# Four graph layers in one launch: row blocks 0 to 2 of layer 3 moved into the end of layer 2

## The chip, the core and the metric

One core of a Trainium2 chip runs the whole program. Its engines work side by side and each takes its instructions in its own order: TensorE (PE, matrix products and transposes), VectorE (DVE), ScalarE (ACT), GpSimd (POOL) and SyncE (SP, which here only issues transfers). They wait for each other through semaphores. The metric is the time of one execution in microseconds (us), as the device measures it.

## The reference, cut to what matters

4096 nodes with 256 features, a dense 0/1 adjacency of 4096 x 4096, four graph layers; each is followed by a residual and a layer norm. The change touches the last two:

```
# layer 2, two steps: R is the row-normalised adjacency with a diagonal,
# A the attention of each row, cut to its top 90% of probability
for n in range(2):
    A  = top_p_attention(Xa, W1, W2, W3)
    Xf = R @ Xf
    Xa = A @ Xa
    Z  = Z + Xf @ U1[n].T + Xa @ U2[n].T
x = layernorm(x + layernorm(x0 + Z) * g + b)

# layer 3
agg = adj @ x / max(deg, 1)
x = layernorm(x + relu(concat([x, agg]) @ W + b))
```

Layer 3 is computed as adj @ (x W_low) and x W_high: the products with W come first, so that what is left per row block is one product of the adjacency with a matrix of 512 columns.

## The kernel before

The rows are taken in 32 blocks of 128. All blocks of one matrix fill one operand, XD, with a high and a low part of 256 columns each (their sum is the value); a product of the adjacency with it takes 32 matmuls of 128 x 128 by 512 for a row block.

Layer 2 runs two steps. In each, a loop over b pipelines several row blocks. For block b + 2 it makes the scores (logits and exponentials, `scores`) and the diffusion (`diffusion`, R @ Xf: eight pieces of the adjacency, 256 KB each, come from DRAM in three buffers, and each serves four matmuls with XD). For block b + 1 it finds the threshold of the attention (`nucleus`, nearly all of it on DVE) and masks the exponentials e with it (line 1145). For block b it turns the masked rows (`turn`, transposes, line 1285, with a copy on ACT) and multiplies them with X (`gather`, line 1294), eight times each. The exponentials of a block fill one of three tiles, e0 to e2, 16 KB on each partition. In step 1, `closing` (POOL, with statistics on DVE) makes h, the block's finished row after two layer norms, of the gathered sum, and `ahead3` multiplies h with the weights of layer 3 (`turned`, line 1378, and `weighted`, line 1387): the half for XD goes to DRAM as xtd, the other with h itself to xo. The order of TensorE, ACT, DVE and POOL in the loop is that in which the code is written out: eight stages s for each b. SP's order is made by a scheduler.

At the end of the loop (b = 30) no new block is begun. `settled` checks on DVE that every row's threshold is exact, and two small transposes (lines 1200 and 1204) bring the answer into one row of flags. It is stored to DRAM, and all engines read it back as a register. If a flag is not set, `mend` makes that block anew in an exact way; with these inputs that branch is not entered. The transposes stand in stage 4, ahead of the last gathers. Behind the loop, block 31 is turned and gathered, closed, and multiplied with the weights of layer 3. `reload` brings the finished rows of all other blocks from xtd into XD: seven loads of 1 MB for blocks 0 to 27, and one for 28 to 30. Block 31's own go from PSUM to XD (lines 1460 and 1462).

Layer 3 keeps the adjacency as bytes (nad) in DRAM. For each 8 row blocks, `bytes_of` loads four tiles of 1 MB over ACT's queue; `adj_pieces` casts them for one block, four pieces of 128 x 1024 by DVE (line 205) and ACT (line 203) in turn. Then come 32 matmuls (line 1647) and `close`: the sum over the degree, the bias, relu, residual and layer norm.

In step 1's diffusion the pieces are those that layer 1 stored, with a one added on the diagonal. The lines named L1158 and L1592 are those of the branch and of the flag's read.

Of the kernel before, what the change touches and what calls it, by code (L numbers as in the profile page):

```python
# [14 lines left out]
U8 = mybir.dt.uint8  # L15
# [40 lines left out]
class Net:  # L56
# [686 lines left out]
    def layer2(self):  # L743
# [3 lines left out]
        with ExitStack() as ctx:  # L747
            pool = ctx.enter_context(tc.tile_pool(name="l2", bufs=1))
            work = ctx.enter_context(tc.tile_pool(name="l2w", bufs=2))
            psum = ctx.enter_context(tc.tile_pool(name="l2ps", bufs=2, space=PSUM))  # L750
            ps1 = ctx.enter_context(tc.tile_pool(name="l2ps1", bufs=1, space=PSUM))
            dram = ctx.enter_context(tc.tile_pool(name="l2d", bufs=1, space=DRAM))
# [7 lines left out]

            es = [pool.tile([P, 4096], F32, name=f"e{i}") for i in range(3)]
            pre = es[0]
# [23 lines left out]
            nc.vector.memset(ones, 1.0)  # L786
            kT = pool.tile([P, N], F32R, name="kT")

# [136 lines left out]

            def product(q, out, **exp):

                e2 = out.rearrange("p (c n) -> p c n", n=1024)
                for c in range(HALF // 512):
                    pl = psum.tile([P, 2, 512], F32, name="ps_logit", bufs=2)  # L930
                    for s in range(2):
                        for t in range(2):
                            nc.tensor.matmul(pl[:, s, :], q[:, t, :], kT[:, (2 * c + s) * 512:(2 * c + s + 1) * 512],  # L933
                                             start=(t == 0), stop=(t == 1))
                    to = e2[:, c]
                    if exp:
                        nc.scalar.activation(to, pl.rearrange("p s n -> p (s n)"), AF.Exp, accum_out=exp["sums"][:, c:c + 1])  # L937
                    else:
                        nc.scalar.copy(to, pl.rearrange("p s n -> p (s n)"))
                    yield  # L940
# [21 lines left out]
            def scores(b, q):  # L962

                zp = small("zp", HALF // 512, bufs=2)
                yield from product(q, es[b % 3][:, :N], sums=zp)
                zj = small("zj", HALF // 512)
                nc.scalar.activation(zj, zp, AF.Identity, accum_out=Zs[:, b:b + 1])
# [186 lines left out]

            def mend(step, row, flag, e, r, h=None):


                with tc.If(flag == 0):  # L1158
                    with tc.For_i(0, NB - 1, 1) as b:
                        with tc.If(nc.values_load(row[:, at(b)], min_val=0, max_val=1) == 0):  # L1160
                            e2, Z = exact_scores(b)
                            r2 = exact_nucleus(e2, Z)
                            if step == 1:
                                finish(b, whole(closing(b, attention(e2), r2, bases(b))))
                            else:
                                store(b, attention(e2), r2)
                    with tc.If(nc.values_load(row[:, NB - 1:NB], min_val=0, max_val=1) == 0):
                        if step == 1:
                            e2, Z = exact_scores(NB - 1)
                            r2 = exact_nucleus(e2, Z)  # L1170
                            nc.scalar.mul(h[:, 0], attention(e2)[:, :D], r2)
                        else:
                            e2, Z = exact_scores(NB - 1, e)
                            nc.vector.tensor_copy(r, exact_nucleus(e2, Z))
                    if step == 1:
                        reload(xtd, 0, NB - 1)

            def settled():
# [18 lines left out]
                nc.vector.tensor_reduce(tmp, tto, AX.X, ALU.max)  # L1197
                nc.vector.scalar_tensor_tensor(ok, tmp, 0.0, ok, op0=ALU.is_equal, op1=ALU.mult)
                pt = psum.tile([P, 512], F32, name="ps_tp")
                nc.tensor.transpose(pt[:NB, :P], ok, self.ident)  # L1200
# [9 lines left out]

            def exact_scores(b, e=None):

                q = work.tile([P, 2, P], F32R, name="q", bufs=2)
                nc.sync.dma_start(q.bitcast(F32), qd[:, :, bass.ds(b * P, P)])
                if e is None:
                    e = es[(NB - 2) % 3][:, :N]
                whole(product(q, e))
# [253 lines left out]
            def weights(step):  # L1471
# [4 lines left out]
                nc.scalar.dma_start(affine, row_broadcast((self.ln_b, self.ln_g)[step], D))  # L1476

            weights(0)
            for step in range(2):
# [33 lines left out]
                with tc.manual_schedule(engines={ET.PE, ET.Activation, ET.DVE, ET.Pool}):  # L1513
                    for b in range(NB - 1):
                        ahead = b + 2 < NB
                        edge = nucleus(step, b + 1, *guess)
                        if ahead:
                            score = scores(b + 2, q)
                            beside = diffusion(step, b + 2)
                        close, kept, put = None, None, None  # L1520
                        for s in range(8):
                            if s == 0:
# [16 lines left out]
                            if step == 1 and b - 2 in done:  # L1539
# [3 lines left out]
                                elif s == 3:  # L1543
                                    pz = weighted(xT, pl[:, 1])
                            if ahead:
                                for _ in range(pieces[s]):
                                    next(beside)
# [31 lines left out]
                            if s == 4 and not ahead:  # L1579
                                row = settled()  # L1580
                            if s < 6:
                                aTs.append(turn(es[b % 3], s + 2))
                            elif ahead:
                                aTs.append(turn(es[(b + 1) % 3], s - 6))
                        if ahead:
                            pr = result(beside)
                            if b + 3 == NB:
                                reload((xfd, xtd)[step], 0, NB - 4)
# [28 lines left out]
                if step == 0:  # L1617
                    nc.scalar.mul(X[:, b, :], pa[:, :D], r)
                    reload(xfd, NB - 4, NB)
                else:  # L1620
                    hand = []
                    close = closing(b, pa, r, bases(b), hand.append)
                    next(close)
                    mend(step, row, flag, None, None, *hand)
                    reload(xtd, NB - 4, NB - 1)
                    finish(b, whole(close), True)

    def layer3(self):
        nc, tc, NB, D = self.nc, self.tc, self.NB, self.D
        G = 8
        with ExitStack() as ctx:
            pool = ctx.enter_context(tc.tile_pool(name="l3", bufs=1))
            work = ctx.enter_context(tc.tile_pool(name="l3w", bufs=2))
            psum = ctx.enter_context(tc.tile_pool(name="l3ps", bufs=4, space=PSUM))
# [6 lines left out]
            nas = []  # L1644

            def product(ps, a, jc):
                nc.tensor.matmul(ps, a[jc // G][:, jc % G, :], self.XD[:, jc].rearrange("p s d -> p (s d)"),  # L1647
                                 start=(jc == 0), stop=(jc == NB - 1))

            def products(b):  # L1650

                ps = psum.tile([P, 512], F32, name="ps_adj")
                a = pieces.pop(b)
                for jc in range(NB - 1):
                    product(ps, a, jc)
                return b, ps, a

            def close(b, ps, a, done=False):
                if not done:
                    product(ps, a, NB - 1)  # L1660
                x = work.tile([P, 2, D], F32, name="x", bufs=3)
# [11 lines left out]


            pieces = {b: self.adj_pieces(work, nas, b) for b in range(2)}
            first = [products(b) for b in range(2)]
            for t in first:
                close(*t)
                pieces[t[0] + 2] = self.adj_pieces(work, nas, t[0] + 2)
            for b in range(2, NB):  # L1680
                t = products(b)
                product(t[1], t[2], NB - 1)
                if b + 2 < NB:
                    pieces[b + 2] = self.adj_pieces(work, nas, b + 2)
                close(*t, done=True)

# [54 lines left out]
```

## Time and profile before

| what | value |
|---|---|
| median of 3 runs | 4110.43 us (4107.63 to 4112.28) |
| the profiled execution | 4113.95 us |
| its span, first to last instruction | 4112.3 us |
| TensorE: matmul busy, weight load busy | 3910.7 us, 3384.7 us |
| DVE, ACT, POOL busy | 3009.2, 2765.0, 1057.6 us |
| layer 3's matmuls, first to last | 3858.05 to 4098.62 us |
| bytes moved | 545.15 MB |

Times in the views count from the span's start. The three runs are of the unprofiled program, and the profiled execution is one more. A view of instructions in order of time gives the start, the busy time, and in brackets how long the engine had been idle before and what released it. A matmul of 32-bit floats is counted as two instructions, and as one where the operands are of the faster 32-bit kind (F32R), as all products with XD are.

### The profile page before, as it was taken

Reading aid. Unit: us, or ns where it says so; the run is one execution under the profiler, and the core shown is the slowest. Engines: PE = TensorE matmul, PEld = TensorE weight load, DVE = VectorE, ACT = ScalarE, POOL = GpSimd, SP = SyncE. Lnnn points to the kernel's source line nnn. Section 1 sums busy time; section 2 is a strip of 40 time slices with the busy share of each in tenths; the row PEclk is TensorE's granted clock in tenths of the full one; section 3 lists DMA queues with packets and bytes.
Section 4 is the critical chain, followed back from the end, with each engine's and each line's share of the span. In section 5 each row is a group of like instructions: output and inputs, shape, how many; then the busy total and the mean of one; then the engine's idle time right before and its main releaser. Section 6 shows DMA issues by size and latency. Waiting matters only on the chain. (4 is left out here: it accounts for less than half of the span.)

```text
span 4112.3 us, 68661 instructions
## 1 busy us (share of the span) xinstructions
PE 3910.7 (95%) x25081; PEld 3384.7 (82%) x25081; DVE 3009.2 (73%) x6659; ACT 2765.0 (67%) x5135; POOL 1057.6 (26%) x1297
## 2 busy tenths in 40 slices
PE   7999989999999899899999999988999999998798
PEld 6899989999999687468888888864888888887687
DVE  7642229999998344657888878846899999999254
ACT  5543339999997322458888888734888888886232
POOL 0111110110333122301111111103465555555110
PEclk9999999999999899899999999989999999999899
DMA  4765555324220597333333233444333333334431
GB/s 120 229 210 177 178 187 169 94 85 147 85 90 26 216 384 270 113 109 99 98 97 101 93 97 98 163 110 135 105 103 109 109 105 118 101 108 157 141 125 43
DMA packets 287962, 545.15 MB, mean 133 GB/s; under 512 B 38294, under 2 KB 118294, under 8 KB 283510
## 3 DMA queue, kind: packets, MB, share of 16 engines
q1 hardware_dynamic: 200068, 367.08, 27.8%
q10 hardware_dynamic: 61154, 93.25, 6.6%
q0 software_dynamic: 26384, 80.24, 5.9%
q8 instruction: 203, 3.33, 0.3%
q14 instruction: 153, 1.25, 0.1%
HBM read 374.51 MB, written 165.94 MB: 131 GB/s over the span
## 5 line engine op out<-in xcount | busy, mean ns | idle before, releaser
L1294 PE MATMUL ps_a<-X,aT 128*128 128x256 f32 x4096 | 974.6, 381 | 2.6 <-ACT h L1435 1.1
L1294 PEld LDWEIGHTS ps_a<-X,aT 128*128 128x128 f32 x4096 | 776.3, 191 | 127.0 <-issue 2.9
L300 PE MATMUL acc<-gm,gt 128*128 128x198 bf16 x8192 | 705.6, 249 | 26.7 <-issue 15.0
L300 PEld LDWEIGHTS <-gt 128*128 128x128 fp8e4 x8192 | 701.8, 97 | 30.4 <-issue 15.2
L292 ACT ACTIVATE sg<-lpb,nlc 128x1024 fp8e4<-128x1024 f32 x640 | 671.4, 1135 | 59.9 <-DVE gt L294 34.8
L179 PE MATMUL ps_r<-XD,adj_piece 128*128 128x512 f32 x2048 | 580.7, 418 | 10.0 <-ACT dif L1332 5.8
L517 PE MATMUL pz<-src,ar 128*128 128x264 f32 x4096 | 509.1, 287 | 11.7 <-DVE ar L507 9.1
L517 PEld LDWEIGHTS pz<-src,ar 128*128 128x128 f32 x4096 | 505.5, 189 | 15.2 <-DVE ar L507 12.8
L1030 ACT ACTIVATE ja<-e,nc 128x2048 uint8<-128x2048 f32 x240 | 480.9, 2004 | 2.0
L1287 ACT COPY aT<-ps_tp 128x512 f32<-128x512 f32 x512 | 295.9, 578 | 228.0 <-PE ps_tp L1285 218.4
L179 PEld LDWEIGHTS ps_r<-XD,adj_piece 128*128 128x128 f32 x2048 | 365.5, 191 | 91.2 <-issue 14.3
L510 ACT ACTIVATE nb<-a 128x512 uint8<-128x512 f32 x256 | 156.4, 630 | 292.4 <-DMA a<-in_adjt_dram 280.7
L1095 DVE MAX8 cand<-v 128x8 f32<-128x256 f32 x1024 | 347.2, 412 | 4.4
L203 ACT ACTIVATE adj_piece<-na 128x1024 fp32r<-128x1024 fp8e4 x128 | 135.3, 1059 | 318.9 <-PE ps_adj L731 134.6
L1145 DVE SCALAR_TENSOR_TENSOR e<-e,edge 128x512 f32<-128x512 f32 x512 | 345.9, 748 | 2.2
L1285 PE MATMUL ps_tp<-ident,e 128*128 128x128 f32 x2048 | 309.8, 274 | 5.3 <-ACTq L1158 3.9
L1285 PEld LDWEIGHTS ps_tp<-ident,e 128*128 128x128 f32 x2048 | 256.4, 141 | 59.0 <-ACTq L1158 4.3
L1091 DVE SCALAR_TENSOR_TENSOR v<-e,hi 128x2048 f32<-128x2048 f32 x128 | 301.9, 2359 | 2.3
L285 DVE TENSOR_SCALAR sg<-lpb,nlc 128x1024 fp8e4<-128x1024 f32 x384 | 283.0, 774 | 2.0
L933 PE MATMUL ps_logit<-kT,q 128*128 128x512 f32 x1024 | 274.7, 409 | 9.1 <-DVE kT L891 3.7
L937 ACT ACTIVATE e<-ps_logit 128x1024 f32<-128x1024 f32 x256 | 259.8, 1025 | 31.5 <-PE ps_logit L933 31.5
L507 DVE CAST ar<-a 128x1024 fp32r<-128x1024 f32 x128 | 88.7, 693 | 232.6 <-PE pz L517 232.3
(348 smaller groups left out, 5539.5 us busy)
## 6 DMA issues: line engine op xcount, KB each, us to landing
adj_piece<-adjs SPq DMA_DIRECT2D x512, 256.0 KB
a<-in_adjt_dram SPq DMA_DIRECT2D x256, 256.0 KB
adjs<-adj_piece SPq DMA_DIRECT2D x96, 512.0 KB
na<-nad SPq DMA_DIRECT2D x64, 512.0 KB
na<-nad ACTq DMA_DIRECT2D x32, 1024.0 KB
nad<-nb POOLq DMA_DIRECT2D x128, 128.0 KB, 3.3
lpb<-lpd POOLq DMA_DIRECT2D x32, 512.0 KB, 4.4
gmd<-gb ACTq DMA_DIRECT2D x64, 198.0 KB
```

The lines of the kernel that those rows point to most:

```text
L179: nc.tensor.matmul(ps, a[:, k, :], rhs(jc).rearrange("p s d -> p (s d)"), start=(jc == 0), stop=(jc == self.NB - 1))
L285: nc.vector.tensor_scalar(sg[:, k, :], lpb, nlc[:, jc, h:h + 1], 2.0 ** -5, op0=ALU.is_ge, op1=ALU.mult, saturate=False)
L292: nc.scalar.activation(sg[:, k, :], lpb, AF.Sign, scale=-1.0, bias=nlc[:, jc, h:h + 1], saturate=False)
L300: nc.tensor.matmul(acc[:, q, :6 * C1], gt[:, k, q * P:(q + 1) * P], gm[:, jc, hh, :], start=(jc == 0 and q % 2 == 0), stop=(jc == NB - 1 a ...
L517: nc.tensor.matmul(pz[q][:, t, :W], ar[:, q, k, :], src[:, jc, t, s], start=(jc == 0 and s == 0), stop=(jc == NB - 1 and s == 1))
L1030: nc.scalar.activation(ja, e[:, s * HALF:(s + 1) * HALF], f, bias=nc1, accum_out=fs[:, i + s:i + s + 1])
L1091: nc.vector.scalar_tensor_tensor(v, ec, hi, ec, op0=ALU.is_lt, op1=ALU.mult, accum_out=sb[:, s:s + 1])
L1095: nc.vector.max(cand[:, 8 * j:8 * j + 8], v[:, k * 256:(k + 1) * 256])
L1145: nc.vector.scalar_tensor_tensor(ec, ec, edge[:, j:j + 1], ec, op0=ALU.is_ge, op1=ALU.mult)
L1285: nc.tensor.transpose(pt[:, k * P:(k + 1) * P], e[:, jc * P:(jc + 1) * P], self.ident)
L1287: nc.scalar.copy(aT, pt)
L1294: nc.tensor.matmul(pa[:, :D], aT[:, k * P:(k + 1) * P], X[:, jc, :], start=(jc == 0), stop=(jc == NB - 1))
```

## The change

- The pools of layer 2 are split. e0 to e2 and kT stay on the left side of the memory and outlive layer 2, as do its PSUM pools; all others move to the right side.
- `settled` gives its DVE part in stage 4 and its transposes after the loop, in both steps.
- In the last iteration of step 1, `early` makes 28 of the 32 matmuls of layer 3's row blocks 0 and 1: two pieces of the adjacency in each stage from the second on. The pieces come over SP's queue, and POOL takes the one off the diagonal again.
- Behind the branch, block 2 is made in the same way, and `cast3` casts block 3 from bytes into kT, all by DVE. The order of this end is written out too. Block 31's last layer norm, its product and the last four matmuls, one of each block, follow.
- The bytes for row blocks 0 to 7 are loaded into e2 and e0, and those for 8 to 15 into X, by SP instead of ACT. Layer 3 begins with block 4, and its sums rotate through the four PSUM banks of layer 2.
- `mend` and `exact_scores` are changed so that the branch leaves these tiles alone and makes blocks 0 and 1 anew.

```
+            self.ctx3 = ExitStack()
+            rows2 = self.ctx3.enter_context(tc.tile_pool(name="l2", bufs=1))
+            pool = ctx.enter_context(tc.tile_pool(name="l2s", bufs=1, side="right"))
+            work = ctx.enter_context(tc.tile_pool(name="l2w", bufs=2, side="right"))
...
-            es = [pool.tile([P, 4096], F32, name=f"e{i}") for i in range(3)]
+            es = [rows2.tile([P, 4096], F32, name=f"e{i}") for i in range(3)]
...
-            kT = pool.tile([P, N], F32R, name="kT")
+            kT = rows2.tile([P, N], F32R, name="kT")
...
                 nc.vector.scalar_tensor_tensor(ok, tmp, 0.0, ok, op0=ALU.is_equal, op1=ALU.mult)
+                yield
                 pt = psum.tile([P, 512], F32, name="ps_tp")
                 nc.tensor.transpose(pt[:NB, :P], ok, self.ident)
...
+            def early(ps, b, groups):
+                for g in groups:
+                    a = work.tile([P, 4, P], F32R, name="adj_piece", bufs=3)
+                    nc.sync.dma_start(a.bitcast(F32), self.adjs[b, :, 4 * g:4 * g + 4, :])
+                    k = b - 4 * g
+                    if 0 <= k < 4:
+                        nc.gpsimd.tensor_sub(a[:, k, :], a[:, k, :].bitcast(F32), self.ident)
+                    for k in range(4):
+                        jc = 4 * g + k
+                        if jc == NB - 1:
+                            yield a
+                        nc.tensor.matmul(ps, a[:, k, :], XD[:, jc].rearrange("p s d -> p (s d)"),
+                                         start=(jc == 4), stop=(jc == NB - 1))
+                    yield
+
+            def both(pairs):
+                for b in range(2):
+                    yield from early(pairs[:, b], b, (1, 2, 3, 4, 5, 6, 0))
...
+                        if step == 1 and not ahead:
+                            pairs = psum.tile([P, 2, 512], F32, name="ps_logit", bufs=2)
+                            beside = both(pairs)
+                            nas = [t[:, i * 2048:(i + 1) * 2048].bitcast(U8).rearrange("p (k i) -> p k i", k=8)
+                                   for t in (es[2], es[0]) for i in range(2)]
+                            self.load_bytes(nas[:2], 0, 0)
+                            pieces = (0, 2, 2, 2, 2, 2, 2, 2)
...
-                            if ahead:
+                            if ahead or step == 1:
                                 for _ in range(pieces[s]):
                                     next(beside)
...
                             if s == 4 and not ahead:
                                 row = settled()
+                                next(row)
...
+                        if not ahead:
+                            row = result(row)
+                            if step == 1:
+                                self.load_bytes(nas[2:], 0, 2)
...
-                    mend(step, row, flag, None, None, *hand)
+                    mend(step, row, flag, None, None, *hand, pairs)
+                    third = ps1.tile([P, 512], F32, name="ps_r")
+                    beside = early(third, 2, (1, 2, 3, 4, 5, 6, 0, 7))
+                    next(close)
                     reload(xtd, NB - 4, NB - 1)
-                    finish(b, whole(close), True)
+                    with tc.manual_schedule(engines={ET.PE, ET.Activation, ET.DVE, ET.Pool}):
+                        for g in range(7):
+                            next(beside)
+                        next(close)
+                        a = [kT[:, i * 1024:(i + 1) * 1024].rearrange("p (k i) -> p k i", k=8) for i in range(4)]
+                        self.cast3(nas, 3, a, nc.vector)
+                        h = whole(close)
+                        rests = [early(pairs[:, k], k, (7,)) for k in range(2)] + [beside]
+                        for t in rests:
+                            next(t)
+                        finish(b, h, True)
+                        for t in rests:
+                            next(t)
+                    self.ahead3 = nas, [X[:, 8 * i:8 * i + 8, :].rearrange("p b d -> p (b d)").bitcast(U8)
+                                        .rearrange("p (k i) -> p k i", k=8) for i in range(4)], a
+                    self.early3 = pairs[:, 0], pairs[:, 1], third
+
+    def load_bytes(self, nas, it, g):
+        for na in nas:
+            self.nc.sync.dma_start(na, self.nad[it, :, 8 * g:8 * g + 8, :])
+            g += 1
+
+    def cast3(self, nas, b, pieces, engine=None):
+        nc = self.nc
+        at = b * P % self.IT
+        for g, (a, na) in enumerate(zip(pieces, nas)):
+            edges = na[:, :, at:at + P].bitcast(FP8)
+            if engine or g % 2 == 0:
+                nc.vector.tensor_scalar_mul(a, edges, 2.0 ** 5)
+            else:
+                nc.scalar.mul(a, edges, 2.0 ** 5)
+        return pieces
...
+            def ready(b):
+                it = b * P // self.IT
+                if b * P % self.IT == 0:
+                    self.load_bytes(nas[it % 2], it, 0)
+                a = [work.tile([P, G, P], F32R, name="adj_piece", bufs=2 * (NB // G)) for _ in range(NB // G)]
+                pieces[b] = self.cast3(nas[it % 2], b, a)
...
-            pieces = {b: self.adj_pieces(work, nas, b) for b in range(2)}
-            first = [products(b) for b in range(2)]
-            for t in first:
-                close(*t)
-                pieces[t[0] + 2] = self.adj_pieces(work, nas, t[0] + 2)
-            for b in range(2, NB):
-                t = products(b)
-                product(t[1], t[2], NB - 1)
+            ready(4)
+            for b, ps in enumerate(self.early3):
+                close(b, ps)
+            for b in range(3, NB):
+                ps = products(b)
                 if b + 2 < NB:
-                    pieces[b + 2] = self.adj_pieces(work, nas, b + 2)
-                close(*t, done=True)
+                    ready(b + 2)
+                close(b, ps)
```

In TensorE's built order, the 31 matmuls of block 3 that don't need block 31 stand mixed among block 2's, ahead of line 1378 for block 31. In POOL's, the subtraction for block 2 stands between lines 1446 and 88 of block 31's closing. In SP's, one load of bytes stands before the last pieces of block 31's diffusion, one behind the reload of XD, two among the early pieces, and the four loads into X among the pieces of block 2.

More of the change, by code (lines that the diff above doesn't have):

```diff
@@ L747, in layer2 @@
         with ExitStack() as ctx:
[L748 to L751, printed above, removed]
+            self.ctx3 = ExitStack()
+            rows2 = self.ctx3.enter_context(tc.tile_pool(name="l2", bufs=1))
+            pool = ctx.enter_context(tc.tile_pool(name="l2s", bufs=1, side="right"))
+            work = ctx.enter_context(tc.tile_pool(name="l2w", bufs=2, side="right"))
+            psum = self.psum2 = self.ctx3.enter_context(tc.tile_pool(name="l2ps", bufs=2, space=PSUM))
+            ps1 = self.ps2 = self.ctx3.enter_context(tc.tile_pool(name="l2ps1", bufs=1, space=PSUM))
             dram = ctx.enter_context(tc.tile_pool(name="l2d", bufs=1, space=DRAM))
@@ L924, in spreads, with product @@
                     nc.vector.tensor_scalar(qsp, spread, CENTRAL[2], CENTRAL[3], op0=ALU.mult, op1=ALU.add)
-            def product(q, out, **exp):
+            def product(q, out, sums):
                 e2 = out.rearrange("p (c n) -> p c n", n=1024)
@@ L934, in product @@
                                              start=(t == 0), stop=(t == 1))
[L935 to L939, printed above, removed]
+                    nc.scalar.activation(e2[:, c], pl.rearrange("p s n -> p (s n)"), AF.Exp, accum_out=sums[:, c:c + 1])
                     yield
@@ L964, in scores @@
                 zp = small("zp", HALF // 512, bufs=2)
-                yield from product(q, es[b % 3][:, :N], sums=zp)
+                yield from product(q, es[b % 3][:, :N], zp)
                 zj = small("zj", HALF // 512)
@@ L1153, in reload, with mend @@
                     nc.sync.dma_start(XD[:, k:to].bitcast(F32), src[k:to].rearrange("b p s d -> p b s d"))
-            def mend(step, row, flag, e, r, h=None):
+            def mend(step, row, flag, e, r, h=None, pairs=None):
+                spare = es[(NB - 2 + step) % 3][:, :N]
                 with tc.If(flag == 0):
@@ L1160, in mend @@
                         with tc.If(nc.values_load(row[:, at(b)], min_val=0, max_val=1) == 0):
-                            e2, Z = exact_scores(b)
+                            e2, Z = exact_scores(b, spare)
                             r2 = exact_nucleus(e2, Z)
@@ L1168, in mend @@
                         if step == 1:
-                            e2, Z = exact_scores(NB - 1)
+                            e2, Z = exact_scores(NB - 1, spare)
                             r2 = exact_nucleus(e2, Z)
@@ L1175, in mend @@
                     if step == 1:
-                        reload(xtd, 0, NB - 1)
+                        reload(xtd, 0, NB - 4)
+                        for k in range(2):
+                            nc.tensor.matmul(pairs[:, k], kT[:, :P], XD[:, 0].rearrange("p s d -> p (s d)"),
+                                             start=False, stop=True)
+                        whole(both(pairs))
             def settled():
@@ L1209, in settled, with exact_scores @@
                 return rowd
-            def exact_scores(b, e=None):
+            def exact_scores(b, e):
                 q = work.tile([P, 2, P], F32R, name="q", bufs=2)
                 nc.sync.dma_start(q.bitcast(F32), qd[:, :, bass.ds(b * P, P)])
-                if e is None:
-                    e = es[(NB - 2) % 3][:, :N]
-                whole(product(q, e))
+                for c in range(N // 512):
+                    pl = bank()
+                    for t in range(2):
+                        nc.tensor.matmul(pl, q[:, t, :], kT[:, c * 512:(c + 1) * 512], start=(t == 0), stop=(t == 1))
+                    nc.scalar.copy(e[:, c * 512:(c + 1) * 512], pl)
                 nb = work.tile([P, 1], F32, name="nb", bufs=1)
@@ L1633, in layer3 @@
         G = 8
[L1634 to L1637, printed above, removed]
+        with self.ctx3 as ctx:
+            pool = ctx.enter_context(tc.tile_pool(name="l3", bufs=1, side="right"))
+            work = ctx.enter_context(tc.tile_pool(name="l3s", bufs=2, side="right"))
             bias = self.load_row(pool, self.b3, "bias3")
@@ L1642, in layer3, with close @@
             out = self.rows(self.out)
[L1644 to L1648, printed above, removed]
+            psum, ps1 = self.psum2, self.ps2
+            *nas, a = self.ahead3
+            pieces = {3: a}
+            def ready(b):
[4 more added lines that the diff above has]
+                pieces[b] = self.cast3(nas[it % 2], b, a)
             def products(b):
-                ps = psum.tile([P, 512], F32, name="ps_adj")
+                if b % 4 < 2:
+                    ps = psum.tile([P, 512], F32, name="ps_tp")
+                else:
+                    ps = ps1.tile([P, 512], F32, name=("ps_r", "ps_a")[b % 2])
                 a = pieces.pop(b)
[L1654 to L1660, printed above, removed]
+                for jc in range(NB):
+                    nc.tensor.matmul(ps, a[jc // G][:, jc % G, :], self.XD[:, jc].rearrange("p s d -> p (s d)"),
+                                     start=(jc == 0), stop=(jc == NB - 1))
+                return ps
+            def close(b, ps):
                 x = work.tile([P, 2, D], F32, name="x", bufs=3)
```

## The prediction

> **What bounds the kernel now.** I read the page's head, the chain that ended last, then TensorE's instructions in order of time at the two ends of layer 2, then all engines in short windows there. The head:
> ```profile
> span 4112.3 us, 68661 instructions
> PE 3910.7 (95%) x25081; PEld 3384.7 (82%) x25081; DVE 3009.2 (73%) x6659; ACT 2765.0 (67%) x5135; POOL 1057.6 (26%) x1297
> ```
> TensorE (PE) is busy 95%, so only its gaps and its total work count. The chain that ended last, in order of time (start, us, what):
> ```profile
> 3842.71 0.70 PE ps_tp L1378 x2
> ...
> 3848.41 2.75 DMA xo<-h
> ...
> 3851.45 4.99 DMA na<-nad
> ...
> 3858.05 240.57 PE ps_adj L1647 x1024
> ```
> Layer 3 is one unbroken run of 1024 matmuls, 240.57/1024 = 0.2349 us each; a block of 32 is 7.52 us, three are 22.6. Ahead of it stand block 31's closing, the store of h and the loads of na. TensorE there (start, us, what, idle before it and its releaser):
> ```profile
> 2684.37 0.37 PE L1200 MATMUL ps_tp<-ident,okay 128*32 128x128 f32 x1 [12.35 <-DVE okay L1198]
> ...
> 2697.31 1.97 PE L1285 MATMUL ps_tp<-ident,e 128*128 128x128 f32 x8 [3.90 <-ACTq L1158]
> ...
> 3798.44 0.37 PE L1200 MATMUL ps_tp<-ident,okay 128*32 128x128 f32 x1 [12.91 <-DVE okay L1198]
> ...
> 3842.71 0.69 PE L1378 MATMUL ps_tp<-ident,h 128*128 128x128 f32 x2 [9.56 <-POOL h L96]
> ...
> 3858.05 22.12 PE L1647 MATMUL ps_adj<-XD,adj_piece 128*128 128x512 f32 x84 [10.35 <-DVE adj_piece L205]
> ```
> In step 1 it idles 12.91 + 9.56 + 10.35 = 32.8 us. Windows of 4 us (width, busy PE, PEld, DVE, ACT, POOL, PE clock, DMA share, GB/s):
> ```profile
> 3768.00:3772.00 4.00, 3.89 (x22) 3.14 (x20) 4.00 (x5) 3.45 (x14) 0.00 (x0) 1.00 1.05 407
> 3772.00:3776.00 4.00, 3.06 (x16) 2.73 (x17) 3.79 (x8) 2.05 (x4) 2.95 (x3) 1.00 1.04 387
> 3776.00:3780.00 4.00, 4.00 (x25) 3.52 (x24) 3.93 (x9) 0.86 (x2) 3.65 (x4) 1.00 0.68 247
> 3788.00:3792.00 4.00, 0.00 (x0) 0.00 (x0) 3.61 (x18) 0.00 (x0) 2.55 (x5) 0.51 0.09 33
> 3836.00:3840.00 4.00, 0.00 (x0) 0.00 (x0) 0.31 (x1) 0.00 (x0) 3.31 (x5) 0.50 0.19 71
> ```
> The reader is to see that the DMA engines are full until 3778.7 (the reload of XD), that VectorE (DVE) sets the first gap, GpSimd (POOL) the second, and that the clock is half after each gap.
>
> **What the skill says.** "DMA: Bandwidth & Descriptors", Issuing engines are not separate DMA queues: queues of all engines share the same 16 DMA engines. The trace agrees: share 1.0 at 387 to 407 GB/s[...]. The same page, Anatomy of one DMA: about 2.0 us fixed for each transfer, mostly the receipt. The trace's 128 KB xo<-h took 2.75 us, so 2.4 fixed at 390 GB/s, which I take: a 256 KB piece lands 3.1 us after its issue, if nothing stands before it. "TensorE: Matmul & The Clock Gate", What's actually happening: an idle window of about 3.4 us halves the clock, as long a busy one restores it; the trace agrees (0.50, 0.51). "Perfetto Trace Analysis", Tensor Engine Instruction (MATMUL, LD_WEIGHTS): ACT, DVE and GpSimd queues are strict FIFO. The trace agrees: DVE L1462, whose inputs were ready at 3782.3, ran at 3786.36 in its place.
>
> **The change, part by part.** *Step 0's end.* The two okay transposes now follow the last three gathers, which TensorE makes in the 12.35 us gap: two turns and three gathers, 2 x 0.45 + 3 x 1.75 = 6.2 us, end 2678. In exchange DVE masks e (5.37) before it reduces each, so row is stored at about 2690.9 instead of 2685.76, flags are read by 2692.6, the branch joins about 0.6 later, and block 31's turns start near 2693.2 instead of 2697.31: -4.1 us. Bounds 0 (ACT's read of the flag took 2.37 us here and may again) and -5.
>
> *Block 30's iteration.* 56 early matmuls, 13.2 us, go into it. The first stand in TensorE's order before gather 1, at 3775.2, but their bytes are on SP's queue behind all of XD. The queue from 3765.9: adj_piece 0.26 MB, four XD loads 4.19, the new nad load into e2 1.05, the first early piece 0.26: 5.77 MB at 390 GB/s is 14.8 us, plus 1 for the other queues and 0.8 of receipt: 3782.5 (at the 305 GB/s of 3764 to 3768, 3786.5). The other new nad load before the reload uses an idle stretch (0 GB/s from 3744 to 3748); the pieces behind it have 3 us to spare. So TensorE stalls 7.3 us, its clock halves, about 2 us more. Behind the stall stands block 28's projection L1387 (now after four early pieces too); ACT copies it, DVE L1462 subtracts it: 3795.8 instead of 3786.36, and all of nucleus(31) behind it on DVE is 9.4 later: okay 3807.7, e masked by 3813.1. TensorE from 3782.5: seven rounds of two pieces, gather, turn (1.95 + 1.75 + 0.45), the projection 2, the cold 2, and about 0.6 for the last piece, which waits for the nad load before it: gather 7 ends at 3816.4, so okay no longer waits. From L1378 (3808.34) to the end of block 31's gathers (3833.14) are 24.8 us; now they begin at 3817.3 and end at 3842.1. That is 9.0 later for 13.2 of work. Bounds +4 (no stall) and +14 (305 GB/s). POOL's two subtractions here (0.46 each, by the row of adj_own) cost nothing: what POOL has next waits for DVE or for gather 7 anyway.
>
> *After the gathers (call their end G).* Before, layer 3 began at G + 24.9. Now: POOL adds to h at G + 1.9, DVE takes block 31's statistics, then casts block 3 (4 x 0.69): TensorE starts at G + 3.3, perhaps at half clock (+1). It does 31 matmuls of block 3, 28 of block 2, then 9 more, 16 us. POOL's order is the catch: the subtraction on block 2's piece 0 (0.46, as adj_own) stands after L1446 and before L88. That piece is the seventh of seven in three buffers, behind two 1 MB loads into X: it is asked for when piece 4 is used, G + 14 to 16, and lands at G + 17 to 19 (a load into X holds the DMA engines 1.05/0.39 = 2.7 us). Then 0.5, then the chain from L88 to L96 (3835.83 to 3842.66, 6.8): L1378 starts at G + 24.3 to 26.3; I take 25.3, instead of G + 9.57. TensorE's own work with its last piece ends at G + 22.7. Transposes, copy and projection, warm: 2.8 (4.9 before). Then four last matmuls under the store of h, since the pool of layer 3's pieces takes the rows of layer 2's: 0.7 + 2.75 of DMA + 0.95 of cast and start, 4.4: block 4 starts at G + 32.5. The 5 us of na loads are gone, hidden under block 31. Bounds G + 29.9 (POOL's stop not felt) and G + 38 (each X load 5 us, as na).
>
> *Layer 3.* 28 blocks x 7.52 = 210.5 us. Per block the same casts, closing, four PSUM banks and eight piece buffers; the closings of blocks 0 to 2 run under blocks 4 and 5 (DVE 52% busy in 3950 to 4000). Cost nothing; without that cover 3 x 4 us at the start. Pools moved to the other side, exact_scores and mend: nothing, neither is in the taken path.
>
> Sum: 3842.1 + 32.5 + 210.5 = 4085.1 against 4098.6, -13.5; with step 0, -17.6. The profiled execution had 4113.95 (1.65 around the span), so 4096.4; the median of the runs stands 3.5 under it, so about **4093**.
>
> **Rivals.** (A) The bytes come in time and POOL's subtraction isn't felt: 4 + 29.9 - 24.9 - 30.1 = -21.1, with -5: -26, 4084. For it: the three gaps hold 32.8 us. Against it: DMA share 1.0 up to 3778.7. (B) The gain is spent: G + 14 and G + 36 give 14 + 36 - 24.9 - 30.1 = -5, step 0 -1: 4104. For it: the X loads stand before the piece that POOL waits for. (C) Slower: layer 3 no longer runs unbroken, because the 28 blocks' first pieces come late (casts behind the three extra closings, the X rows read by SP's loads). At 0.9 us a block it costs 25: 4118; it decides above 17.6/28 = 0.63 us a block. Against it: TensorE waits 0 us in layer 3 now, with DVE half idle. (D) The change does not act: if the blocks were late as a whole, TensorE would do them after L1378 and 0 be gained; the built order excludes it.
>
> **Numbers.** Forecast 0.57, A 0.18, B 0.15, C 0.07, D 0.03. A measurement tells 0.2% (8.2 us) from no change. Faster: forecast, A and a quarter of B, 0.79; same: most of B and D, 0.13; slower 0.08. The range, 4083 to 4107, takes in A and B; the forecast's own is 4087 to 4100.
>
> **What would show it.** L1200 of step 0 with block 31's turns 3 to 5 us earlier; a gap of 5 to 11 us before the first early matmul, ended by a DMA; DVE L1462 about 9 us later than its neighbours' old place; a POOL stop before L88 of some 14 us, ended by a DMA; one unbroken run of 896 matmuls of 210 us. Wrong would be: no gap before the early matmuls, POOL's subtraction under 1 us late, or idle TensorE within the last 210 us.

## The result, and the profile after

The changed kernel takes 4102.33 us (median of 20 executions, 4097.6 to 4110.0) against 4109.92 us for the kernel before beside it: a ratio of 0.9981, 95% interval 0.9974 to 0.9988, or 7.6 us less. A second comparison, beside other kernels, gave 0.9987 (0.9981 to 0.9994). The forecast was 17.5 us less.

Absolute positions can't be compared between two executions: the first gather of block 30 in step 0 stands at 2661.36 us in the profile of before and at 2656.30 in that of after, and no instruction has moved up to there. So I compare four stretches, each from one of TensorE's instructions to another (G is the end of block 31's gathers in step 1, as in the prediction):

| stretch | before | after, two profiles | change forecast |
|---|---|---|---|
| step 0: block 30's first gather to block 31's first turn | 35.95 | 35.24, 35.03 | -4.1 |
| step 1: block 30's first gather to G | 60.20 | 70.37, 70.79 | +9.0 |
| G to the first matmul of layer 3 proper (block 4; before: block 0) | 24.9 | 38.6, 37.8 | +7.6 |
| from there to TensorE's end | 240.6 | 211.9, 211.8 | -30.1 |

The measured changes add up to -0.8 + 10.4 + 13.3 - 28.7 = -5.8 us, about what the medians say. Most of the gain is missing from the first stretch (3.3 us) and the third (5.7); the second and the fourth each fall 1.4 us short of what was forecast.

The page's head for the changed kernel, to be read beside that of before:
```profile
span 4101.3 us, 68724 instructions
PE 3911.0 (95%) x25081; PEld 3380.8 (82%) x25081; DVE 3002.8 (73%) x6655; ACT 2757.6 (67%) x5127; POOL 1062.5 (26%) x1300
```
TensorE has as much work as before, and its share has not risen: the change has moved its gaps. Its instructions in order of time show where to (start, us, what, the idle time before it and who ended it):
```profile
2679.25 0.37 PE L1204 MATMUL ps_tp<-ident,okay 128*32 128x128 f32 x1 [6.23 <-DVE okay L1201]
2684.71 0.21 PE L1208 MATMUL ps_tp<-ident,each 32*1 32x32 f32 x1 [5.09 <-DVE each L1206]
2691.54 1.94 PE L1291 MATMUL ps_tp<-ident,e 128*128 128x128 f32 x8 [6.63 <-DVE e L850]
...
3777.53 3.75 PE L1498 MATMUL ps_logit<-XD,adj_piece 128*128 128x512 f32 x8 [8.26 <-DMA adj_piece<-adjs]
```
At step 0 two gaps, of 12.35 and 3.90 us, have become three, of 6.23, 5.09 and 6.63. In block 30's iteration the first early matmul waits 8.26 us for its bytes and then runs at half clock (3.75 us for 8 matmuls, where later ones take 2.11), as forecast. What follows G is read from the chain of work that ended last:
```profile
3840.44 5.51 PE ps_a L1738 x16
...
3852.45 5.20 DMA adj_piece<-adjs
...
3859.82 5.29 DMA adj_piece<-adjs
...
3865.16 1.65 PE ps_r L1498 x3
3866.81 0.44 PE ps_tp L1384 x2
...
3867.76 3.69 PE ps_tp L1393 x4
...
3872.14 2.73 DMA xo<-h
...
3875.79 17.73 PE ps_tp L1738 x64
```
Two pieces of block 2 take 5.2 and 5.3 us each from issue to landing, one after the other, because the second is asked for only when the first one's matmuls have given their buffer back; the transposes of h (L1384) stand behind both, at G + 29.6. SyncE's queue says what the pieces stand behind:
```profile
3849.16 0.42 SPq L1693 DMA_DIRECT2D X<-nad  x1
3852.45 2.19 SPq L1490 DMA_DIRECT2D adj_piece<-adjs  x3
3854.69 0.42 SPq L1693 DMA_DIRECT2D X<-nad  x1
3859.82 0.32 SPq L1490 DMA_DIRECT2D adj_piece<-adjs  x1
```
A 1 MB load of layer 3's next bytes into X goes out ahead of each, and the fourth such load 0.37 us behind the last piece. Those bytes are first read when block 8 is cast, at 3895.5, some 20 us after block 4 has begun. Behind that nothing is open: layer 3's 28 blocks run without a gap (7.47 us each, the first two slower at a clock not yet back).

### The profile page after: what moved, and what is told of

It reads as the page before. It is cut to its first block, busy times and chain, and to the rows that moved or that the text cites. A ratio compares the mean times of both kernels' runs of the same rounds, so it can differ in the third digit from the quotient of the medians.

```text
span 4101.3 us, 68724 instructions
## 1 busy us (share of the span) xinstructions
PE 3911.0 (95%) x25081; PEld 3380.8 (82%) x25081; DVE 3002.8 (73%) x6655; ACT 2757.6 (67%) x5127; POOL 1062.5 (26%) x1300
## 3 DMA queue, kind: packets, MB, share of 16 engines
q8 instruction: 203, 3.33, 0.3%
## 5 line engine op out<-in xcount | busy, mean ns | idle before, releaser
L292 ACT ACTIVATE sg<-lpb,nlc 128x1024 fp8e4<-128x1024 f32 x640 | 671.3, 1135 | 60.3 <-DVE gt L294 34.8
L731 PE MATMUL ps_adj<-XD,adj_piece 128*128 128x512 f32 x1024 | 236.1, 391 | 0.0
```

The costliest lines, as they stand in the source:

```text
L292: nc.scalar.activation(sg[:, k, :], lpb, AF.Sign, scale=-1.0, bias=nlc[:, jc, h:h + 1], saturate=False)
```

## The experiments

Three theories share the 9 us that are missing from the first and the third stretch. **Loads**: the four loads into X delay block 2's late pieces, and everything stands behind these. **POOL**: GpSimd's subtraction on piece 0, which stands before L88, holds the closing of block 31 (the prediction's step). **Branch**: at step 0 the skipped repair (mend) itself costs TensorE time, which ScalarE's late flag hid before. Each run's profile gives the stretches of the table; a ratio is good to about 0.07% (3 us) with some 20 executions and 0.13% (5 us) with 5 or 6. A stretch comes from one profile of each kernel, so it is to be read beside its scatter, which is given below.

### Step 0: back to the old order, and a short body to jump over

The first kernel undoes the change at step 0 alone:
```
                             if s == 4 and not ahead:
                                 row = settled()
-                                next(row)
+                                if step == 0:
+                                    row = whole(row)
+                                else:
+                                    next(row)
...
-                            row = result(row)
                             if step == 1:
+                                row = result(row)
```


> The changed kernel with step 0's settled() put back where it was (whole at s == 4, both transposes among the gathers); all else as changed. I measure the stretch from the first gather of step 0's block 30 to the first turn of block 31: 35.95 us before the change, 35.24 after it. Theory (TensorE's own branch over mend, 3.7 us in the trace, was hidden behind ScalarE's late flag before and is bare now): the stretch goes back to about 35.9, +0.7 us, a ratio to the changed kernel that can't be told from 1. The prediction's step (4.1 us gained at step 0's end): +4.1 us.

The stretch is 36.03 us, against 34.9 to 35.3 in nine profiles with the change's order; the ratio, 0.9986 (0.998 to 0.9993), can't tell such a difference. So the change's reordering at step 0 is worth about 0.9 us, not 4.1.

Where the rest went is seen in the records of the If at L1157, here in the changed kernel (engine, operation, count: ns least/median/most, when):
```profile
L1157 DVEq EVENT_SEMAPHORE  x2: 21/21/21, 2690.3 to 2690.4; - x2
L1157 PEldq EVENT_SEMAPHORE  x2: 51/51/51, 2691.1 to 2691.3; - x2
L1157 ACTq COMPARE_BRANCH  x1: 54/54/54, 2687.2 to 2687.2; - x1
...
L1157 DVEq COMPARE_BRANCH  x1: 72/72/72, 2687.3 to 2687.3; - x1
L1157 PEldq COMPARE_BRANCH  x1: 3688/3688/3688, 2687.3 to 2687.3; - x1
```
All engines reach the branch at 2687.2 to 2687.3, as early as the prediction had it (its 2692.6 less 5.1 of drift). But TensorE's branch lasts 3.69 us, and VectorE's next instruction comes 3.0 us after its own. Before the change the same branch took as long and nobody saw it (the view of L1158 in the kernel before):
```profile
L1158 PEldq COMPARE_BRANCH  x1: 3728/3728/3728, 2691.5 to 2691.5; - x1
...
L1158 ACTq COMPARE_BRANCH  x1: 54/54/54, 2696.8 to 2696.8; - x1
```
ScalarE, the last, branched only at 2696.8. To see whether the length of the skipped code matters:
```
 def mend(step, row, flag, e, r, h=None, pairs=None):
     spare = es[(NB - 2 + step) % 3][:, :N]
+    if step == 0:
+        with tc.If(flag == 0):
+            pt = bank()
+            nc.tensor.transpose(pt[:, :P], self.ident, self.ident)
+            nc.scalar.copy(e[:, :P], pt[:, :P])
+            nc.vector.tensor_copy(r, e[:, :1])
+            nc.gpsimd.tensor_copy(e[:, 1:2], r)
+            nc.sync.dma_start(xad[0], e[:, :D])
+        return
     with tc.If(flag == 0):
```


> The changed kernel, in which step 0's mend has one small instruction for each engine under its If instead of the repair of flagged rows (the repair is left out; its flag is still stored, read and branched on by all five engines). Branch theory: the 3.7 us of TensorE's branch and the 3.0 us between VectorE's branch and its next instruction are the jump past a long body; with a short one both fall below 1 us and the first turn of block 31 comes 2.5 to 3.3 us earlier in the stretch from the first gather of block 30 (35.24 now, about 32.3 then). Rival (the store of row, its landing and the read of the flag are what costs): the stretch stays within 0.5 us of 35.24.

```profile
L1158 PEldq COMPARE_BRANCH  x1: 232/232/232, 2688.0 to 2688.0; - x1
```
TensorE's branch falls from 3.69 to 0.23 us and the stretch to 31.75: 3.4 us less, somewhat more than expected. The Trainium skill names a mechanism that fits in "Runtime: NRT & Kernel Launch", Instruction fetch mechanics: a taken branch whose target lies outside the instructions already fetched has to fetch them first. The traces agree: in the changed kernel the only DMA packets between 2687.2 and 2690.5 are three of instructions, 8, 8 and 16 KB, begun some 1.0 us after the branch; with the short body no packet begins from 2687.9 to 2689.5. The section gives no price; here it is 3.3 to 4.0 us on TensorE and 2.8 to 3.5 on VectorE. The medians (ratio 0.9981, 0.9974 to 0.9987) can't tell 3.4 us from nothing; the stretch can.

A version that keeps the repair hides the mask beside store, flag and branch:
```
-                            if s < 6:
+                            if s < (6 if ahead or step else 5):
                                 v = result(edge)
...
                             row = result(row)
+                            if step == 0:
+                                rs[b + 1] = result(edge)
```


> The changed kernel, in which step 0's VectorE takes each and row before it masks block 31's e (in the changed kernel the mask, 5.4 us, stands before them); TensorE still makes its last gathers first. Theory (at step 0's end two things stood in a row: the mask, and behind it the store of row, the flag and TensorE's 3.7 us branch): with row stored 5.2 us earlier the mask lies beside store, flag and branch, and the stretch from step 0's first gather of block 30 to the first turn of block 31 falls from 35.1 (35.0 to 35.3 in five profiles) to 30 +- 1 us, what the prediction hoped from the change's own reordering. Rival (another engine joins late anyway): 34 us or more.

```profile
2688.13 1.94 PE L1291 MATMUL ps_tp<-ident,e 128*128 128x128 f32 x8 [6.18 <-PEq L1157]
```
The stretch is 30.07 us (-5.0), and what releases the turn is now TensorE's own branch (PEq), which takes 3.51 us here. The ratio is 0.9976 (0.9969 to 0.9984).

### After G: the loads into X

Behind the pieces (xs are the rows of X as layer 3 names them; ready(8) then loads nothing):
```
-with tc.manual_schedule(engines={ET.PE, ET.Activation, ET.DVE, ET.Pool}):
+with tc.manual_schedule(engines={ET.PE, ET.Activation, ET.DVE, ET.Pool, ET.SP}):
...
     for t in rests:
         next(t)
+    self.load_bytes(xs, 1, 0)
     finish(b, h, True)
```


> The changed kernel with SyncE in the fixed order of the last part, and the four 1 MB loads into X issued after the ten pieces of adjs instead of between them (they are first read by block 8). Stretch from the end of block 31's gathers (G) to block 4's first matmul: 38.6 us in the changed kernel. Theory (pieces stand behind the 1 MB loads): a late piece lands 3 us after its issue instead of 5.2 to 5.3, TensorE's two waits for pieces (2.71 and 3.40) shrink to about 0.5 and 1.2, the projection runs warm: 38.6 becomes 32 to 34, -5 us. Rival (GpSimd's order holds the closing, or TensorE's own work is the bound): -1 us or less.

G to block 4 is 34.5 us, and TensorE's transposes come at G + 22.4 (29.6 in the changed kernel):
```profile
3868.99 0.69 PE L1384 MATMUL ps_tp<-ident,h 128*128 128x128 f32 x2 [1.52 <-POOL h L96]
...
3877.17 1.22 PE L1498 MATMUL ps_logit<-XD,adj_piece 128*128 128x512 f32 x2 [3.20 <-DVE XD L1468]
```
The seven later pieces land 2.6 to 3.5 us after their issue, and TensorE's two waits for pieces have gone to nothing and 0.60. TensorE's built order has changed too, though not by hand: eight matmuls of block 3 that stood ahead of the seventh piece's request now stand behind it, an estimated 1.9 us at 0.235 us each. But the ratio is 0.9988 (0.9981 to 0.9994), no better than the changed kernel's, and only about half of the 7 us gained at the transposes arrives at block 4. ScalarE, in order of time:
```profile
3868.96 0.34 ACTq L1460 DMA_DIRECT2D xo<-h  x1
3869.77 0.37 ACT L1386 COPY xT<-ps_tp 128x256 f32<-128x256 f32 x1 [22.67 <-PE ps_tp L1384]
3874.01 0.37 ACT L1466 CAST XD<-ps_tp 128x256 fp32r<-128x256 f32 x1 [3.87 <-PE ps_tp L1393]
3876.29 0.37 ACT L1467 COPY h<-ps_tp 128x256 f32<-128x256 f32 x1 [1.90 <-DMA xo<-h]
```
When the first store of h (L1460, on ScalarE's own queue) goes out, 2.7 MB of the four loads are still to be moved: the store takes 7.3 us, and the copy L1467, which overwrites h, waits for it, then VectorE's L1468, and TensorE for that (3.20 us above). The delay has moved from the pieces to the store.

POOL alone:
```
-    for g in range(7):
+    for g in range(6):
         next(beside)
     next(close)
...
     h = whole(close)
+    next(beside)
```


> The changed kernel with GpSimd's subtraction on block 2's piece 0 put behind the whole closing chain of block 31 (L88 to the second L96) instead of before it; loads and TensorE's order as they are. Theory (pieces behind the 1 MB loads, and TensorE's transposes of h stand behind the matmuls that wait for them): the closing is done some 10 us earlier and nobody uses it, G to block 4 stays within 1 us of 38.6. Rival (the prediction's step: GpSimd's stop before L88 sets the transposes): G to block 4 falls by 4 us or more.

Its closing is done at G + 11.0 (the second L96 ends at 3853.50), 17 us earlier than in the changed kernel, and nobody uses it: TensorE stands at the pieces, as in the changed kernel.
```profile
3869.61 1.65 PE L1498 MATMUL ps_r<-XD,adj_piece 128*128 128x512 f32 x3 [3.44 <-DMA adj_piece<-adjs]
```
G to block 4 is 38.2 us, ratio 0.9982 (0.9974 to 0.999). POOL alone gives nothing that can be told from the scatter.

The loads out of the way of pieces and stores, behind the second store of h on SyncE's queue, first without and then with POOL's move:
```
-    finish(b, h, True)
+    whole(ahead3(b, h, weighted(turned(h[:, 0], bank()), bank()), True, nc.sync))
+    self.load_bytes(xs, 1, 0)
```


> The changed kernel with the four 1 MB loads into X out of the way altogether: SyncE in the fixed order, all ten pieces, then the second store of h, then the loads into X. Nothing else moved by hand. Theory (the loads delay first the pieces and, when put behind them, the first store of h, for which ScalarE's copy of h waits: 34.5 us in the kernel with the loads only behind the pieces): both are gone, TensorE's transposes of h come at about G + 22.4 (then GpSimd's order is what they wait for), and G to block 4's first matmul is 31 +- 1.5 us, against 37 to 39. Rival (the stretch is held by other things and scatters by itself): 35 us or more.

> The last kernel with GpSimd's subtraction behind the closing as well. Theory (once the loads are gone, GpSimd's place is the next bound, by some 1.5 us, and TensorE's own work the one after it): transposes of h at G + 20.5 to 21.5, G to block 4 another 1 to 1.5 us shorter, about 30. Rival (GpSimd's order costs nothing): as the last kernel to within 0.5 us.

Without POOL's move: 34.8 us, not 31 and barely under the rival's 35; ratio 0.9977 (0.9969 to 0.9984). The pieces now land in time, and the transposes wait for POOL, to G + 25.25:
```profile
3866.10 0.44 PE L1384 MATMUL ps_tp<-ident,h 128*128 128x128 f32 x2 [2.21 <-POOL h L96]
```
The granted clock is halved behind the stall, and the projection takes 3.58 us. With POOL's move as well: 29.85 us, the transposes at G + 22.0, ratio 0.9969 (0.9958 to 0.9981), the projection warm at 1.99. My split was wrong, the sum right: POOL's place costs some 4 to 5 us once the loads are gone, not 1 to 1.5, and about 3 go to the loads. While both stand, either hides the other: POOL's move alone gave nothing.

Three things blur this split. TensorE's order is the one with eight matmuls of block 3 moved back, in both kernels, so up to an estimated 1.9 of the 3 us for the loads may be that order's. Then, the first 16 matmuls of block 3 stand behind a gap of 3.2 to 3.5 us in every profile and take 3.9 us where the clock stays full, as in the kernel with the loads only behind the pieces, and up to 6.7 where it is halved. They took 6.69 us without POOL's move and 5.49 with it; the seventh piece is asked for, and POOL released, later by as much. That is why the transposes came at G + 25.25 and not at the 22.4 that I had expected, and an estimated 1.2 us of the 5 is this and not POOL's place. And in these two kernels layer 3 is no longer unbroken: TensorE stands 1.1 and 2.2 us there for casts. In the first, VectorE waits 7.05 us for a load of x that goes out while the loads into X are under way; that this is the cause was not tested.

### Block 30's stall, and the last part ordered anew

The changed kernel was run once more beside these, for the scatter:

> The changed kernel itself once more, as the neighbour of the next three and for a second profile: how far do its stretches scatter from one profiled execution to another. Expected: first gather of step 1's block 30 to the end of block 31's gathers (G) 69 to 71 us, G to block 4's first matmul 35 to 40 us (38.6 in its first profile; 35.7 and 39.6 in the two kernels so far that differ from it only at step 0), and a ratio to the kernel before of 0.998 to 0.9985.

It did as expected (70.79 and 37.75 us, ratio 0.9987). The ten profiles with the changed kernel's block 30 give 68.8 to 72.5 us for that stretch, the six with its last part 35.7 to 39.6 us from G to block 4.

Then the early pieces of block 30:

```
-pieces = (0, 2, 2, 2, 2, 2, 2, 2)
+pieces = (0, 0, 0, 2, 3, 3, 3, 3)
```


> The changed kernel with the early pieces of block 30's iteration begun three gathers later: pieces (0, 0, 0, 2, 3, 3, 3, 3) instead of (0, 2, 2, 2, 2, 2, 2, 2). Theory (the early matmuls stand in TensorE's order before the bytes can be there, and the projection of block 28, which VectorE waits for, stands behind that stall): the 8 us stall falls below 2, VectorE's search for block 31 is no longer late, and the stretch from block 30's first gather to G falls from 70 to 60 +- 2 us, the time by some 9 us. Rival (the 13.2 us of early matmuls are TensorE's own time wherever they stand): the stretch stays within 2 us of 70.

```profile
3782.25 2.90 PE L1498 MATMUL ps_logit<-XD,adj_piece 128*128 128x512 f32 x8 [1.95 <-DMA adj_piece<-adjs]
```
The stall is 1.95 us instead of 7.4 to 8.9, the stretch 63.3 us instead of 70, the ratio 0.9971 (0.9959 to 0.9983). Not 60: TensorE's waits for pieces later in the iteration (1.5 and 1.0 us) remained. Of 13.2 us of early matmuls some 10 now lie in time that TensorE would have waited, since the stretch is 3.1 us longer than before the change.

The last part, ordered anew (its core; the pieces of block 2 lie in eight rows, so that none waits for a buffer):
```
+last = rows2.tile([P, 4096], F32R, name="e1")
+rows = [last[:, i * 512:(i + 1) * 512].rearrange("p (k i) -> p k i", k=4) for i in range(8)]
+beside = early(third, 2, (1, 2, 3, 4, 5, 6, 0, 7), rows)
...
     h = whole(close)
+    block3(0, 16)
+    next(beside)
+    xT = turned(h[:, 0], bank())
+    next(beside)
+    pz = weighted(xT, bank())
+    rests = [early(pairs[:, k], k, (7,)) for k in range(2)]
     for t in rests:
         next(t)
+    whole(ahead3(b, h, pz, True))
+    next(beside)
     for t in rests:
         next(t)
+    for g in range(5):
+        next(beside)
+    next(beside)
+    block3(16, NB)
+    self.load_bytes(xs, 1, 0)
```
block3(lo, hi) makes the matmuls of block 3 for column blocks lo to hi, which layer 3 then leaves out.

> The changed kernel with its last part ordered anew: block 2's eight pieces go into the rows of the third e tile (no waiting for one of three buffers), SyncE in the fixed order with the four 1 MB loads into X behind all pieces, GpSimd's subtraction behind the closing, and on TensorE 16 matmuls of block 3 and 8 of block 2, with block 31's transposes and projection among them, before the rest, so that the store of h and the release of layer 2's rows lie under 36 matmuls. Theory (the pieces behind the byte loads, and the closing, the store and the first casts standing one after the other at the end, are what makes 38.6 us): G to block 4's first matmul becomes 25 +- 1.5 us, -11 to -13. Rival (layer 3's own start, its casts and the release of rows, is the bound whatever stands before it): 32 us or more.

> Both of the last two edits together. If the two stages are independent: block 30's first gather to block 4's first matmul falls from about 108 to 85 +- 3 us, and the time to 20 to 23 us below the changed kernel, a ratio to the kernel before of 0.9925 to 0.994. If one only moves the wait into the other: no better than the better of the two.

The last part alone gives 32.0 us and a ratio of 0.9966 (0.9954 to 0.9979), 7 us short of what I expected and just at the rival's 32; with block 30's edit 30.1 and 0.9955 (0.9941 to 0.9969). The two stretches together fall from 108 to 93, not 85. Block 4 now follows without a gap, so the rival's bound (casts, release of rows) is not it. In the second kernel ScalarE, and TensorE behind it, show the largest wait:
```profile
3844.40 0.34 ACTq L1460 DMA_DIRECT2D xo<-h  x1
...
3852.29 0.37 ACT L1467 COPY h<-ps_tp 128x256 f32<-128x256 f32 x1 [4.36 <-DMA xo<-h]
```
```profile
3853.18 0.92 PE L1498 MATMUL ps_logit<-XD,adj_piece 128*128 128x512 f32 x2 [3.33 <-DVE XD L1468]
```
The same copy of h waits for the same store, 7.9 us this time, behind pieces and loads; TensorE loses 3.33 us to it, and 1.44 more before the transposes to POOL's closing. So in the last kernel the copy has a tile of its own:
```
 def ahead3(b, h, pz, last=False, queue=nc.scalar):
...
+    if last:
+        h = work.tile([P, 1, D], F32, name="h", bufs=3)
     nc.scalar.copy(h[:, 0], pz[:, :D])
```
and all that paid goes together (the code puts two more pieces of block 2 ahead of the transposes than the kernel tail has, not one):

> All edits that paid, together: row before the mask at step 0; early pieces from the fourth gather on; the last part ordered anew as in the kernel tail, but with the copy of h into a tile of its own (it waited 4.4 us for the first store of h), one more piece of block 2 ahead of the transposes, and the loads into X behind the second store. If the theory holds in each place: stretches of 30 +- 1, 63 +- 1.5 and 25 +- 1.5 us instead of 35.1, 70.4 and 37.7, some 25 us together, a time of 4078 +- 4 us and a ratio to the kernel before of 0.9915 to 0.993. Rival (a gain in one place is given back in the next): no better than 4085.

The stretches are 30.3, 60.2 and 23.3 us, the time 4078.66 us, a ratio of 0.9924 (0.991 to 0.9938): 31 us less than before the change and some 25 less than with it. The first stretch and the time came out as expected, the other two shorter than their ranges. TensorE's end of it, and the head:
```profile
3831.51 5.51 PE L1684 MATMUL ps_a<-XD,kT 128*128 128x512 f32 x16 [3.22 <-DVE kT L1726]
3836.86 2.90 PE L1500 MATMUL ps_r<-XD,e 128*128 128x512 f32 x12
3839.59 0.38 PE L1384 MATMUL ps_tp<-ident,h 128*128 128x128 f32 x2
...
3851.62 4.60 PE L1761 MATMUL ps_tp<-XD,adj_piece 128*128 128x512 f32 x19
```
```profile
PE 3904.9 (96%) x25081; PEld 3379.9 (83%) x25081; DVE 3003.2 (74%) x6655; ACT 2755.7 (68%) x5127; POOL 1060.9 (26%) x1300
```
After the 3.22 us that VectorE's casts take there is no idle TensorE left between G and its last matmul. Block 30's stretch is as long as before the change, with 13.2 us more work in it; but the two other kernels with these pieces gave 63.3 and 63.1, and nothing else in this stretch was edited, so the last 3 us are scatter until they are seen again. Of how the copy's own tile and the other edits of the last part share the 7 us between 30.1 and 23.3, no run tells.

## Why the prediction was right and wrong

- **Step 0's end, -4.1: wrong (-0.8).** The step that failed is "the branch joins about 0.6 later". VectorE's mask, the row's store and the flag came as worked out, but TensorE's branch past mend takes 3.7 us, and the first turn stands 4.3 us behind the flag's read. The branch stood in the trace of before, ended 1.6 us ahead of ScalarE's, and I took the join for ScalarE's alone.
- **Block 30's iteration, +9.0: right in its mechanism, 1.4 us short (+10.2 and +10.6).** The stall of 7.3 us measured 8.3 and 8.9; VectorE's L1462 (L1468 after the change) came 10.5 later against block 30's first gather, for 9.4 forecast; okay no longer waits. That the projection stands behind the stall was right and was what moving the pieces undid. (The terms given for TensorE add up to 3816.2, not 3816.4; nothing hangs on it.)
- **After G, G + 32.5: wrong (38.6 and 37.8, at the edge of the bounds).** The mechanism, late pieces behind the loads into X, was named; three terms failed. A late piece was to land some 3 us after its issue; it took 5.2 and 5.3, twice in a row (2.6 to 3.5 once the loads were behind it). The prediction put POOL as the bound at G + 25.3 and TensorE's own end at G + 22.7; with these loads POOL is done at G + 27.9 and TensorE's own end is G + 29.6. And "transposes, copy and projection, warm: 2.8" fell with it: it measured 4.6, with the projection behind an idle TensorE at half clock, 3.7 us for 1.9. The 4.4 us from the projection's end to block 4 were right (4.3).
- **POOL's stop before L88: there, but covered.** It lasted 18.7 us, for 14 forecast, ended by a DMA as said. TensorE didn't wait for it in the changed kernel's first profile, and 0.4 and 1.1 us where only an earlier stretch was altered; with the loads gone it put the transposes at G + 25.25. That this is the prediction's 25.3 is in part luck: the prediction had the loads in place, and the slow first matmuls of that profile are in the figure.
- **Layer 3, 210.5: nearly (211.9 and 211.8).** It is unbroken, so rival C is out; block 4 begins cold (17.73 us for 64 matmuls, 15.1 in the last kernel).

What came out, 4102.3 us, lies nearest to rival B, the gain spent, at 4104, with its G + 36 and its -1 at step 0. Its sum of -6 is met in part by luck: block 30 cost 3.6 us less than its +14, and the two last stretches together 3.5 us more.

## What to carry to other kernels

When work is moved under a gap, look at what each queue brings forward into the same time: here loads that nobody needed for 35 us took, by being early, first the pieces' and then the store's place. Where two waits end within a few us of each other, removing one may show almost nothing, as here, and a short result of a single edit doesn't clear its cause; remove both before judging. And read the join of a branch on every engine, not on the last one only: what ended 1.6 us earlier was the next bound here.

## What was not expected of the hardware

- A branch over a long body took TensorE 3.3 to 4.0 us in every profile here (3.33 in step 1 of the kernel before, 3.67 after), and 0.23 us over a body of a few instructions. ScalarE, GpSimd and SyncE show 45 to 54 ns either way. VectorE shows 56 to 72 ns, and then 2.8 to 3.5 us until its next wait for a semaphore behind the long body (0.17 behind the short one).
- Reading the flag took ScalarE 2.37 us at step 0 of the kernel before and 0.47 in step 1; no run tells why.
- A 128 KB store took 2.7 us where hardly anything else was under way (the second store of h in the changed kernel), and 7.3 and 7.9 us with 2 to 3 MB of loads ahead of it on another engine's queue.
